# Grouping full-array and 64-column matmuls of two attention steps into one: a cross-attention and mixture-of-experts kernel

## Chip, cores and metric

One core of a Trainium2 chip (trn2). The metric is device time in microseconds of one execution, as the median of several runs. All times below are microseconds unless they are marked ns. Engines: PE is TensorE, DVE VectorE, ACT ScalarE, POOL GpSimd, and SP the engine whose queue issues most of the transfers.

## What is computed

All arrays are fp32. `x` is 16 batches of 100 rows of 256; `ctx_768` is 16 batches of 361 rows of 192.

```python
def _L0_xattn_ref(x, y, Wq, Wkv, Wproj, bproj):        # H, DK = 16, 64
    q = (x @ Wq).reshape(b, lq, H, DK).transpose(0, 2, 1, 3)
    kv = (y @ Wkv).reshape(b, lkv, 2, H, DK).transpose(2, 0, 3, 1, 4)
    k, v = (kv[0], kv[1])
    atten = jax.nn.softmax(jnp.einsum('bhid,bhjd->bhij', q, k) * SCALE, axis=-1)
    res = jnp.einsum('bhij,bhjd->bhid', atten, v)
    return res.transpose(0, 2, 1, 3).reshape(b, lq, H * DK) @ Wproj + bproj
...
x = x + _L0_xattn_ref(_layernorm(x, axis=-1), ctx_768, ...)
x = x + _L0_ffn_ref(_layernorm(x, axis=-1), ...)
```

`_L0_ffn_ref` is a SwiGLU of inner size 704 that all tokens share, plus one of 7 experts of the same size for each token, chosen by a sigmoid router. The change does not touch it.

## The kernel before

The 1600 tokens are 13 tiles of 128 rows (the last has 64), in groups for the layer norms. `acc` holds x, `xT` the transposed normalised rows. Behind the attention come the shared FFN's remaining groups, the sorting of tokens by expert, and 15 expert tiles; nothing of that is edited.

**Steps.** Attention runs over 32 steps `(b, g)`: 16 batches `b`, each with a first step `g = 0` (heads 0 to 7) and a second `g = 1` (heads 8 to 15). In a step, `scores` (L612) makes four pairs of products of queries with keys (L618): two heads at a time, in the upper and the lower 64 rows of the array, each into its own PSUM bank. For each pair `exponentials` (L629) takes row maxima on DVE (L631) and exponentials with sums on ACT (L634); `turning` (L642) then takes reciprocals (L644) and turns 32 x 32 blocks on DVE (L647) into `tb`. It runs one pair behind the scores, so that the last pair is turned at the end of the step. `moved` (L658) copies the sums' row to DRAM and back (`row`, `over`) and regroups `tb` to `aT` with 16 transfers (L668), half from SP's queue and half from POOL's. One step later `values` (L680) multiplies `aT` with the values `v` (L689: two heads side by side, in 64 columns of the array each) and DVE scales the result into `resT` (L704).

**Other PE work in the steps.** First steps have the batch's three value pairs (`value_pairs` L589, products at L551), second steps the next batch's four key pairs (`key_pairs` L562, also L551). Both are row-tiled: two products of 64 rows side by side. Each pair leaves a `put` that copies two PSUM banks to SBUF, by ACT, or by ACT and DVE. Queries are made for two batches at a time in four units (`q_units` L518, matmul L527, copy by DVE L534). `project` (L711, matmul L716) multiplies `resT` of a finished tile with Wproj and adds it to `acc` (L719). A group's layer norm is a list of small parts for DVE: moments (L171, L172) per tile, roots (L176, and L177 on POOL), normalisation (L182) per tile. Its `turn` (L196) transposes the tiles on PE (L202) and copies them to `xT` on ACT (L205). The router's logits are L232. These use the whole array.

**What orders the work.** PE, ACT, DVE and SP are scheduled by hand in the attention: each engine executes in the order of the calls. Deques feed the steps. `norms` holds layer-norm and router parts (`part`, L745, runs one: after the turned pairs in the step, and one at the end), `turns` holds transposes, `fillers` projections and router calls, `puts` the copies out of PSUM. The loop over the steps (L780) takes from them at fixed places. `load_later` (L488) issues weights and tiles of x by step number, and normalises tiles whose x has come. All PE outputs share one pool of 8 PSUM banks, `ps`, taken in turn, so a product waits until the bank used eight banks earlier has been read. `ap2` gives two buffers to `aT`, `tb`, `over`, `v` and `cT`, three to `kT`.

The functions that the diff touches, and those around them:

Of the kernel before, what the change touches and what calls it, by code (L numbers as in the profile page):

```python
# [22 lines left out]
B, LQ, C = 16, 100, 256  # L23
# [11 lines left out]
QB, QR = 4, 25  # L35
# [9 lines left out]
WE = 2 * 2 * I + (NI + 1) * C  # L45
QG = 2
HG = 8
WARM = 7
ZERO = 8
SAME = 3  # L50
EPS = 1e-5
# [3 lines left out]
def xattn_moe(  # L55
# [16 lines left out]
    nc = tc.nc  # L72
# [381 lines left out]
    with ExitStack() as attn:  # L454
# [22 lines left out]
        cTs = {0: load_ctx(0, NR)}  # L477
# [29 lines left out]
        for i in range(NA):  # L507
            at = aw.tile([P, 2, NJ * P], F32, name=f"at{i}")
            nc.gpsimd.memset(at[:, :, LKV:], 0.0)
            ats.append(at)  # L510
        for i in range(2):
            qT = aw.tile([P, NCH, QG * QB, 32], F32, name=f"qT{i}")
            nc.gpsimd.memset(qT, 0.0)
            qT_bufs.append(qT)

        qTs, kTs, vs, resTs = {}, {}, {}, {}
# [1 line left out]
        def q_units(g):  # L518

            qT = qT_bufs[g % 2]  # L520
            qTs[g] = qT

            def unit(u):
                pq = bank()[:, : 2 * QG * LQ].rearrange("p (o n) -> p o n", o=2)
                for o in range(2):
                    for k in range(2):
                        nc.tensor.matmul(  # L527
                            pq[:, o, :],
                            wq_sb[:, u, k, ts(o, P)],
                            xT[:, k, ts(g, QG * LQ)],  # L530
                            start=(k == 0),
                            stop=(k == 1),
                        )
                nc.vector.tensor_scalar(  # L534
                    qT[:, 2 * u : 2 * u + 2, :, :QR],
                    pq.rearrange("p o (i n) -> p o i n", n=QR),
                    DK**-0.5,
                    None,
                    ALU.mult,
                )  # L540

            return [lambda u=u: unit(u) for u in range(NU)]
# [19 lines left out]
        def key_pairs(b):  # L562
            cT = cTs[b]
            halves = []
            kTs[b] = halves

            def keys(u):


                def operands(o, k):  # L570
                    r = ts(o, P // 2)
                    return wk_sb[r, u, k, :], cT[r, k, :LKV]

                if u % 2 == 0:
                    halves.append(ap2.tile([P, 4, LKV], F32, name="kT", bufs=3))
                kT = halves[u // 2]
                to = pair(operands, P, LKV)

                def put():
                    c = 2 * (u % 2)  # L580
                    nc.scalar.copy(kT[:, c, :], to[0][:, :LKV])
                    one = nc.scalar.copy if u % 2 else nc.vector.tensor_copy
                    one(kT[:, c + 1, :], to[1][:, :LKV])

                return put

            return [lambda u=u: keys(u) for u in range(NU)]

        def value_pairs(b):  # L589
            cT = cTs.pop(b)  # L590
            v = ap2.tile([P, NJ, H * DK], F32, name="v")
            vs[b] = v

            def values_of(j):
                n = keys_in(j)

                def operands(o, k):
                    r = ts(o, P // 2)
                    return cT[r, k, ds(j * P, n)], wv_sb[r, k, :]

                to = pair(operands, n, 512)

                def put():
                    nc.scalar.copy(v[:n, j, :512], to[0][:n, :])
                    one = nc.vector.tensor_copy if j == 1 else nc.scalar.copy
                    one(v[:n, j, 512:], to[1][:n, :])

                return put

            return [lambda j=j: values_of(j) for j in range(NJ)]  # L610
# [69 lines left out]
        def values(b, g, aT, over):  # L680

            n2 = HG // 2
            av = bank()[:, : n2 * LQ].rearrange("p (c n) -> p c n", n=LQ)
            for i in range(n2):
                c = g * n2 + i
                for j in range(NJ):
                    n = keys_in(j)
                    for o in range(2):
                        nc.tensor.matmul(  # L689
                            av[ts(o, DK), i, :],  # L690
                            vs[b][:n, j, ds((2 * c + o) * DK, DK)],
                            aT[:n, :, j, o, ts(i, QR)],
                            start=(j == 0),
                            stop=(j == NJ - 1),
                        )
            blocks = av.rearrange("p c (i n) -> p c i n", n=QR)
            for t in range(b * LQ // P, ((b + 1) * LQ - 1) // P + 1):

                i0 = max(0, t * P - b * LQ) // QR
                i1 = (min(LQ, (t + 1) * P - b * LQ) + QR - 1) // QR  # L700
                if t not in resTs:
                    resTs[t] = ap2.tile([P, NCH, QP + P + QP], F32, name="resT")
                to = resTs[t][:, ts(g, n2), ds(QP + b * LQ + i0 * QR - t * P, (i1 - i0) * QR)]
                nc.vector.tensor_tensor(  # L704
                    to.rearrange("p c (i n) -> p c i n", n=QR),
                    blocks[:, :, i0:i1, :],
                    over[:, i0:i1].rearrange("p i c n -> p c i n"),
                    ALU.mult,
                )
# [13 lines left out]
        turns, fillers, norms = deque(), deque(), deque()  # L723
# [21 lines left out]
        def part():  # L745
            if norms:
                norms.popleft()()

        def after_values():
            if biases:  # L750
                t = biases.popleft()
                nc.gpsimd.tensor_tensor(acc[:, t, :], acc[:, t, :], bp_sb, ALU.add)

        puts = deque()

        def product(pairs):

            puts.append(pairs.pop(0)())
            if len(puts) > 1:
                puts.popleft()()  # L760

        pairs = key_pairs(0)
        product(pairs)
        product(pairs)
        parts, turn_first = layer_norm(FIRST)
        for one in parts:
            one()
        product(pairs)
        product(pairs)
        turn_first()  # L770
        normalised(SECOND)
        qs = q_units(0)
        for _ in range(2):
# [2 lines left out]
        NG = H // HG  # L776
        n2 = HG // 2
        steps = [(b, g) for b in range(B) for g in range(NG)]
        held = None
        for s, (b, g) in enumerate(steps):  # L780
            if g == 0:
                pairs = value_pairs(b)
                if s == 0:
                    kept = [pairs.pop()]
                    ask = lambda: qs.pop(0)() or (lambda: None)
                    pairs[1:1] = [ask, ask]
            elif b + 1 < B:
                pairs = key_pairs(b + 1)
                if s == 1:
                    pairs = kept + pairs  # L790
                if (b + 1) % QG == 0:
                    qs = q_units((b + 1) // QG)
            else:

                hT0 = ap2.tile([P, NJ, H * DK], F32, name="v")
                hT0 = hT0.rearrange("p j n -> p (j n)")[:, : (NI + 1) * 3 * P]
                hT0 = hT0.rearrange("p (i n) -> p i n", i=NI + 1)
                first = hidden(GROUPS[0], hT0, ap2, 3 * P, SAME)
                pairs = [lambda: first.pop(0)() or (lambda: None) for _ in range(SAME)]
            tb = new_blocks()  # L800
            turning = None
            for i in range(n2):
                exponentials, then = scores(b, g * n2 + i)
                if puts:
                    puts.popleft()()
                exponentials()
                if turning:
                    turning(tb)
                    part()
                turning = then  # L810
                if pairs:
                    puts.append(pairs.pop(0)())
            while pairs:
                product(pairs)
            if puts:
                puts.popleft()()
            if turns:
                turns.popleft()()
            if s and fillers:
                fillers.popleft()()  # L820
            for _ in range(min(2, len(qs))):
                qs.pop(0)()
            turning(tb)
            part()
            if s:
                values(b1, g1, *held)
                after_values()
                if g1 == NG - 1:
                    finished(b1)
            held = moved(tb)  # L830
            b1, g1 = b, g
            if g == NG - 1 and b + 2 < B:
                cTs[b + 2] = load_ctx(b + 2)
            load_later(s)
# [6 lines left out]
            if fillers:  # L841
                fillers.popleft()()
        down(GROUPS[0][:2], hT0)
        values(b1, g1, *held)
        down(GROUPS[0][2:], hT0[:, :, 2 * P :])
        finished(b1)
        while fillers:
            fillers.popleft()()

# [196 lines left out]
```

## Time and profile before

| what | value |
|---|---|
| median of 3 runs | 731.54 (731.47 to 731.96) |
| profiled execution, its own time | 730.98 |
| its span on the core | 729.3 |
| mean granted PE clock | 0.998 |
| PE busy, DVE busy, ACT busy | 99%, 58%, 38% of the span |
| L551 PE, value products | 576 records, 131.6, mean 589 ns |
| L551 PE, key products | 768 records, 128.4, mean 465 ns |
| L618 PE, scores | 512 records, 103.1, mean 478 ns |
| L689 PE, attention times values | 1536 records, 75.2, mean 252 ns |
| L527 PE, queries | 256 records, 47.2, mean 337 ns |
| L716 PE, projection | 208 records, 47.8, mean 383 ns |
| L634 ACT, exponentials | 256 records, 142.1, idle before them 206.8, of which 206.6 for DVE nm L631 |

How to read it: an fp32 matmul stands as two records[...]. Records of row-tiled or column-tiled pairs overlap in time[...], so record lengths add up to more than the time they took; starts are the safer measure. "64\*128" after a matmul is the array's part that it uses, rows by columns. In a timeline line stand the start, the time covered, the engine, the line, the operation, output from input, and in brackets the engine's idle time before it with what ended it. In a table of windows each engine has its busy time and its number of instructions; PEclk is the clock granted to PE as a share of full speed, then come the share of time of the DMA engines and GB/s.

### The profile page before, as it was taken

Reading aid. Unit: us, or ns where it says so; the run is one execution under the profiler, and the core shown is the slowest. Engines: PE = TensorE matmul, PEld = TensorE weight load, DVE = VectorE, ACT = ScalarE, POOL = GpSimd, SP = SyncE. Lnnn points to the kernel's source line nnn. Section 1 sums busy time; section 2 is a strip of 40 time slices with the busy share of each in tenths; the row PEclk is TensorE's granted clock in tenths of the full one; section 3 lists DMA queues with packets and bytes.
Section 4 is the critical chain, followed back from the end, with each engine's and each line's share of the span. In section 5 each row is a group of like instructions: output and inputs, shape, how many; then the busy total and the mean of one; then the engine's idle time right before and its main releaser. Section 6 shows DMA issues by size and latency. Waiting matters only on the chain. (4 is left out here: it accounts for less than half of the span.)

```text
span 729.3 us, 14750 instructions
## 1 busy us (share of the span) xinstructions
PE 721.5 (99%) x5206; PEld 516.7 (71%) x5206; DVE 421.2 (58%) x1086; ACT 280.3 (38%) x795; POOL 201.7 (28%) x418
## 2 busy tenths in 40 slices
PE   9999999999999999999999999999999999999996
PEld 6667666676666767576676666756767678999996
DVE  2877668568786866857866695776247222222221
ACT  2554556344544544534534463453021101112111
POOL 5242322323323222422223322223020102543221
PEclk9999999999999999999999999999999999999999
DMA  7164655534655553644534554445103901888860
GB/s 256 47 153 113 178 138 134 129 98 127 174 148 126 147 134 85 162 111 126 137 85 126 119 157 111 109 97 121 58 26 109 419 32 48 317 334 344 308 255 23
DMA packets 54375, 107.95 MB, mean 148 GB/s; under 512 B 28631, under 2 KB 35930, under 8 KB 52368
## 3 DMA queue, kind: packets, MB, share of 16 engines
q1 hardware_dynamic: 43648, 80.51, 36.4%
q0 software_dynamic: 10352, 25.98, 14.2%
q8 instruction: 44, 0.72, 0.4%
q14 instruction: 43, 0.35, 0.2%
q10 hardware_dynamic: 288, 0.39, 0.2%
HBM read 60.39 MB, written 5.35 MB: 90 GB/s over the span
## 5 line engine op out<-in xcount | busy, mean ns | idle before, releaser
L634 ACT ACTIVATE at<-mm,nm 128x361 f32<-128x361 f32 x256 | 142.1, 561 | 206.8 <-DVE nm L631 206.6
L668 POOL DMA_DIRECT2D aT<-tb x256 | 126.4, 501 | 300.1 <-PE mm L689 168.4
L631 DVE TENSOR_REDUCE nm<-mm 128x1 f32<-128x361 f32 x256 | 124.0, 526 | 50.9 <-PE mm L618 49.7
L647 DVE STREAM_TRANSPOSE tb<-at 128x384 f32<-128x384 f32 x256 | 132.9, 558 | 4.8 <-DMA aT<-tb 0.6
L551 PE MATMUL mm<-wv_sb,cT 64*128 64x512 f32 (+1 forms) x576 | 131.6, 589 | 0.0
L551 PE MATMUL mm<-cT,wk_sb 64*128 64x361 f32 x768 | 128.4, 465 | 0.0
L551 PEld LDWEIGHTS mm<-cT,wk_sb 64*128 64x128 f32 x768 | 76.3, 188 | 41.4 <-issue 0.5
L618 PE MATMUL mm<-kT,qT 64*128 64x361 f32 x512 | 103.1, 478 | 0.0
L551 PEld LDWEIGHTS mm<-wv_sb,cT 64*128 64x128 f32 (+1 forms) x576 | 53.9, 181 | 57.3 <-issue 46.5
L929 PE MATMUL mm<-xgT,wex 128*128 128x128 f32 x660 | 78.3, 275 | 0.5 <-ACT xgT L922 0.5
L929 PEld LDWEIGHTS mm<-xgT,wex 128*128 128x128 f32 x660 | 76.9, 192 | 1.4 <-issue 0.7
L689 PEld LDWEIGHTS mm<-aT,v 128*64 128x64 f32 (+1 forms) x1536 | 68.9, 135 | 10.6 <-issue 10.6
L689 PE MATMUL mm<-aT,v 128*64 128x100 f32 (+1 forms) x1536 | 75.2, 252 | 0.0
L618 PEld LDWEIGHTS mm<-kT,qT 64*128 64x128 f32 x512 | 46.6, 185 | 38.7 <-issue 14.4
L402 PE MATMUL mm<-xT,w_sb 128*128 128x384 f32 (+1 forms) x176 | 60.9, 503 | 0.0
L402 PEld LDWEIGHTS mm<-xT,w_sb 128*128 128x128 f32 x176 | 32.9, 190 | 25.7 <-issue 8.5
L634 ACT ACTIVATION_READ_ACCUMULATOR at<-mm,nm 128x1 f32 x256 | 50.4, 197 | 0.0
L527 PE MATMUL mm<-xT,wq_sb 128*128 128x200 f32 x256 | 47.2, 337 | 0.7 <-ACT xT L205 0.7
L716 PE MATMUL mm<-wp_sb,resT 128*128 128x256 f32 (+1 forms) x208 | 47.8, 383 | 0.0
L527 PEld LDWEIGHTS mm<-xT,wq_sb 128*128 128x128 f32 x256 | 43.0, 190 | 4.7 <-issue 2.0
L716 PEld LDWEIGHTS mm<-wp_sb,resT 128*128 128x128 f32 (+1 forms) x208 | 37.7, 186 | 9.9 <-ACT at L634 2.5
L941 PE MATMUL mm<-wex,hgT 128*128 128x256 f32 x180 | 41.4, 380 | 0.0
(139 smaller groups left out, 555.2 us busy)
## 6 DMA issues: line engine op xcount, KB each, us to landing
wex<-in_wex SPq DMA_DIRECT2D x15, 2176.0 KB
aT<-tb POOLq DMA_DIRECT2D x256, 80.2 KB, 3.1
aT<-tb SPq DMA_DIRECT2D x256, 80.2 KB
cT<-in_ctxT SPq DMA_DIRECT2D x15, 541.5 KB
over<-row SPq DMA_DIRECT2D x64, 100.0 KB
xn_d<-xn SPq DMA_DIRECT2D x12, 128.0 KB
base_d<-acc SPq DMA_DIRECT2D x12, 128.0 KB
w_sb<-in_w SPq DMA_DIRECT2D x4, 352.0 KB
```

The source lines that it names most:

```text
L402: nc.tensor.matmul(to[:, :n], w13_sb[:, k, ds(at, P)], xT[:, k, ds(g[0] * P, n)], start=(k == 0), stop=(k == 1),)
L527: nc.tensor.matmul(pq[:, o, :], wq_sb[:, u, k, ts(o, P)], xT[:, k, ts(g, QG * LQ)], start=(k == 0), stop=(k == 1),)
L551: nc.tensor.matmul(to[o][:height, :width], *operands(o, k), start=(k == 0), stop=(k == NR - 1),)
L618: nc.tensor.matmul(sc[o][:, :LKV], qTs[b // QG][r, c, ts(b % QG, QB), :], kTs[b][c // 4][r, c % 4, :], start=True, stop=True,)
L631: nc.vector.tensor_reduce(nm[:, o : o + 1], sc[o][:, :LKV], AX.X, ALU.max, negate=True)
L634: nc.scalar.activation(at[:, o, :LKV], sc[o][:, :LKV], AF.Exp, bias=nm[:, o : o + 1], accum_out=sums[:, o : o + 1],)
L647: nc.vector.transpose(tb[:, :, :, o, i * QR : i * QR + 32].rearrange("p j k n -> p k j n"), at[:, o, :].rearrange("p (k j n) -> p k j n", ...
L668: queue.dma_start(aT[ts(j, 32), i].rearrange("p k o n -> p (k o n)"), tb[ts(i, 32), j].rearrange("p k o n -> p (k o n)"),)
L689: nc.tensor.matmul(av[ts(o, DK), i, :], vs[b][:n, j, ds((2 * c + o) * DK, DK)], aT[:n, :, j, o, ts(i, QR)], start=(j == 0), stop=(j == NJ ...
L716: nc.tensor.matmul(pp[:r, :C], resT[:, c, QP : QP + r], wp_sb[:, c, :], start=(c == 0), stop=(c == NCH - 1))
L929: nc.tensor.matmul(to[:, ts(o, P)], w[:, ds(j * 2 * I + u, P)], xgT[:, j, :], start=(j == 0), stop=(j == 1),)
L941: nc.tensor.matmul(y[:, :C], hT[:, c, :], w[:, ds(4 * I + c * C, C)], start=(c == 0), stop=(c == NI))
```

## The change

It moves calls in the step loop and edits what feeds them:

- Queries, transposes, projections, router logits and the values products now stand only at the end of first steps. There `values` runs for both steps of the batch in front, one after the other (`held` keeps two sets of `aT` and `over`). Second steps have scores, key pairs and value pairs only.
- Of a batch's three value pairs, two are made in the second step of the batch in front, put among its key pairs; the third stays behind the first scores of the batch's first step. Batch 0 makes all three in its first step.
- With more pairs than scores in a step, pairs are spread over the remaining scores, and a pair's `put` is called at the next pair.
- Transposes still run at most once a step, `fillers` until none is left; the query units of batches 2k and 2k+1 are made in the first steps of batches 2k-1 and 2k.
- In the first two steps up to three layer-norm parts run at the end of the step instead of one.
- Ahead of the steps, the first transposes stand before the fourth key pair instead of behind it, one of seven warm-up matmuls goes, and POOL clears only the padding columns of `qT`.
- In the last step no projection is made; tile 10's is made after it, and both of batch 15's values blocks stand together in the tail.

```diff
-WARM = 7
+WARM = 6
...
-            nc.gpsimd.memset(qT, 0.0)
+            nc.gpsimd.memset(qT[:, :, :, QR:], 0.0)
...
         def value_pairs(b):
-            cT = cTs.pop(b)
+            cT = cTs[b]
...
         product(pairs)
+        turn_first()
         product(pairs)
-        turn_first()
         normalised(SECOND)
...
-        held = None
+        held = []
+        values_of = {b: value_pairs(b) for b in (0, 1)}
         for s, (b, g) in enumerate(steps):
             if g == 0:
-                pairs = value_pairs(b)
+                pairs = values_of.pop(b)
                 if s == 0:
-                    kept = [pairs.pop()]
                     ask = lambda: qs.pop(0)() or (lambda: None)
-                    pairs[1:1] = [ask, ask]
+                    pairs[1:] = [ask, ask] + pairs[1:]
+                elif (b + 1) % QG == 0 and b + 1 < B:
+                    qs = q_units((b + 1) // QG)
             elif b + 1 < B:
+                if b:
+                    values_of[b + 1] = value_pairs(b + 1)
                 pairs = key_pairs(b + 1)
-                if s == 1:
-                    pairs = kept + pairs
-                if (b + 1) % QG == 0:
-                    qs = q_units((b + 1) // QG)
+                for i in (4, 2):
+                    pairs.insert(i, values_of[b + 1].pop(0))
...
                 turning = then
-                if pairs:
-                    puts.append(pairs.pop(0)())
-            while pairs:
-                product(pairs)
+                for _ in range(-(-len(pairs) // (n2 - i))):
+                    product(pairs)
             if puts:
                 puts.popleft()()
-            if turns:
-                turns.popleft()()
-            if s and fillers:
-                fillers.popleft()()
-            for _ in range(min(2, len(qs))):
-                qs.pop(0)()
+            if g == 0:
+                if turns:
+                    turns.popleft()()
+                while fillers:
+                    fillers.popleft()()
+                for _ in range(min(2, len(qs))):
+                    qs.pop(0)()
             turning(tb)
-            part()
-            if s:
-                values(b1, g1, *held)
-                after_values()
-                if g1 == NG - 1:
-                    finished(b1)
-            held = moved(tb)
-            b1, g1 = b, g
+            for _ in range(3 if s < 2 else 1):
+                part()
+            if g == 0 and s:
+                for at in range(NG):
+                    values(b - 1, at, *held.pop(0))
+                    after_values()
+                finished(b - 1)
+            held.append(moved(tb))
...
         down(GROUPS[0][:2], hT0)
-        values(b1, g1, *held)
+        for at in range(NG):
+            values(B - 1, at, *held.pop(0))
         down(GROUPS[0][2:], hT0[:, :, 2 * P :])
-        finished(b1)
+        finished(B - 1)
```

## What the change is expected to do

> **What bounds the kernel now.** I read the busy shares first, then TensorE's timeline step by step, then VectorE and ScalarE in the same stretches, last the waits. The page:
>
> ```profile
> PE 721.5 (99%) x5206; PEld 516.7 (71%) x5206; DVE 421.2 (58%) x1086; ACT 280.3 (38%) x795; POOL 201.7 (28%) x418
> PEclk9999999999999999999999999999999999999999
> ```
>
> TensorE (PE) is busy throughout at full clock. So a change can gain only where PE streams less densely, and every wait it puts on PE counts whole. PE's timeline in one first step (here without queries):
>
> ```profile
> 349.73 2.35 PE L689 MATMUL mm<-aT,v 128*64 128x100 f32 x48
> 352.00 0.88 PE L618 MATMUL mm<-kT,qT 64*128 64x361 f32 x4
> 352.71 2.74 PE L551 MATMUL mm<-wv_sb,cT 64*128 64x512 f32 x12
> 355.29 0.77 PE L618 MATMUL mm<-kT,qT 64*128 64x361 f32 x4
> 355.89 2.74 PE L551 MATMUL mm<-wv_sb,cT 64*128 64x512 f32 x12
> ...
> 361.65 0.77 PE L618 MATMUL mm<-kT,qT 64*128 64x361 f32 x4
> 362.36 2.35 PE L689 MATMUL mm<-aT,v 128*64 128x100 f32 x48
> ```
>
> Starts matter. Scores before a value pair take 0.60 (355.29 to 355.89), as inside a row-tiled run. Before L689 they take 0.71 (361.65 to 362.36), after L689 0.71 too (352.00 to 352.71). The excess appears wherever the array's tiling changes: R = 64 rows (L551, L618), C = 64 columns (L689), F = full (L202, L527, L716, L232, L402). From single records' starts (a slot is one record, or the two that run side by side): L689's slots are 0.088 apart, but 0.181 lie between its last and L618's first; L618's are 0.303 apart, but its first two after a change 0.408. So leaving a mode costs about 0.095 and the first slot of the next 0.105 more (0.055 for L689 and L202): 0.15 to 0.20 a change.
>
> Now the engines behind scores, at the end of a first step:
>
> ```profile
> 332.57 0.77 PE L618 MATMUL mm<-kT,qT 64*128 64x361 f32 x4
> ...
> 333.37 0.97 DVE L631 TENSOR_REDUCE nm<-mm 128x1 f32<-128x361 f32 x2 [1.03 <-PE mm L618]
> 334.00 0.56 ACT L634 ACTIVATE at<-mm,nm 128x361 f32<-128x361 f32 x1 [0.16 <-DVE nm L631]
> 334.26 0.16 DVE L644 RECIPROCAL at<-sums 128x2 f32<-128x2 f32 x1
> ...
> 335.00 0.20 ACT L634 ACTIVATION_READ_ACCUMULATOR at<-mm,nm 128x1 f32 x1
> ...
> 338.12 0.16 DVE L644 RECIPROCAL at<-sums 128x2 f32<-128x2 f32 x1
> 338.31 1.04 DVE L647 STREAM_TRANSPOSE tb<-at 128x384 f32<-128x384 f32 x2
> 339.27 0.14 DVE L250 TENSOR_SCALAR lg<-lg 128x21 f32<-128x21 f32 x1
> ```
>
> This gives the units: reduction starts 0.80 after the scores; a reduced pair occupies DVE 0.89 (333.37 to 334.26); a turned pair 1.15 (338.12 to 339.27); ACT's exponentials end 1.83 after the reduction's start (335.20).
>
> **What is removed.** In the new instruction order, mode changes fall from 103 to 67. C to R 30 to 15 at 0.20 (-3.0); R to C 9 to 0 at 0.15 (-1.35); F to C 25 to 18 at 0.15 (-1.05); R to F 28 to 23 (0.20 each, 0.15 to L202, 0.12 to L232) -0.93; F to R one more and C to F one fewer cancel. Sum **-6.3**. The number of matmuls is unchanged but for one warm-up.
>
> At the start, xT's wait goes:
>
> ```profile
> 13.27 0.59 ACT L205 COPY xT<-mm 128x512 f32<-128x512 f32 x1 [1.95 <-PE mm L202]
> 13.91 2.97 PE L527 MATMUL mm<-xT,wq_sb 128*128 128x200 f32 x16 [0.68 <-ACT xT L205]
> ```
>
> A key pair (1.82) now covers it. But the transposes, moved up to 10.8, meet the second L182, done at 11.16: new wait 0.25, plus a mode change already counted. Queries start near 13.58: **-0.3**. The dropped warm-up is worth nothing, since this L182 sets the resumption; without that cover 0.2 [...]. The smaller qT memset is off every path (old one done at 9.54, scores at 16.81).
>
> **What is moved, and who gets late.** In a first step, three scores now stand back to back behind one value pair (2.58). Let 0 be the step's start: scores at 0, 3.18, 3.79, 4.39; PE reaches the full-array work at 5.1. DVE's order is reduce 1, turn 0, norm part, reduce 2, turn 1, norm part, reduce 3, turn 2. Reduce 1 starts at 3.98, turn 0 ends 6.02; without parts reduce 2 ends 6.91, turn 1 8.06, and ACT has exponentials 3 at 9.89. L205's copy stands behind those on ACT, and L182 inside that DVE chain. Before, scores were spread through the step and neither was late. A transposed tile costs PE 0.22, L716 3.46, L182 0.40, a moments part (L171, L172) 0.55, copy to matmul 0.64 (13.27 to 13.91). I resolved the semaphores on which these PE instructions wait in the new program:
> - Batch 1: queries wait for the xT copy just made: 9.95+0.64=10.6, PE ready at 6.05: 4.5.
> - Batch 5: same, two moments parts delay it to 11.7; L716 brings PE to 9.3: 2.4.
> - Batch 6: the fourth transpose waits for L182 after turn 0 (6.5, not 5.8): 0.7.
> - Batch 7: one L182 in the chain; the router's L232 waits for xT until 11.0, PE ready at 9.3: 1.7.
> - Batches 10 and 14: the third transpose waits for the L182 after turn 1: 6.02+0.40+0.89+1.15+0.40=8.86, with handover 8.95; PE there at 5.6: 3.35 each, 6.7.
> Sum **+16.0**. These are lower-bounded by DVE's own busy time, hence ±1.5.
>
> Other queues. aT's copy, from row issue to landing, took 7.5 to 8.5 in every step. The second step now ends with a value pair instead of L689, so the row leaves 1.1 after the next step starts and lands at 8.6 to 9.6; the second L689 block comes at 8.75 in batch 15 (no queries): 0 to 0.9, taken 0.4. Batch 2 has 10.2: free. SP's next ctx transfer lands about 12.1 after the row against a need at 13.1: 0 to 0.3, taken 0.1. The first half's aT copy now waits on SP and POOL for its buffer's L689 at the step's end; behind it stand over, ctx and L177, none needed for several us: nothing. In second steps a value pair adds 0.69 to DVE and 1.77 to ACT, but DVE's 11 and ACT's 10.6 stay below PE's 14.9: nothing. At the tail L716 moves behind L402, still covered: nothing. Waits: **+16.5**.
>
> **The clock.** Nothing in the stretch shows what such idle gaps do to PE's clock (its largest gap here is 0.68). Nearest is the end of the run:
>
> ```profile
> 720.00:724.00 4.00, 3.76 (x18) 2.97 (x16) 0.69 (x2) 0.00 (x0) 0.99 (x1) 1.00 0.11 39
> 724.00:729.00 5.00, 0.00 (x0) 0.00 (x0) 0.28 (x1) 0.00 (x0) 0.98 (x1) 0.70 0.08 26
> ```
>
> PE stops at 723.76; a mean of 0.70 over the next row is full clock for 2.0 and half for 3.0, so the clock halves near 726.0, 2.3 after the last matmul. [...] By the row, batch 1 triggers it and batches 10 and 14 (3.35 with 0.2 of transposes inside) mostly, batch 5 sometimes. [...] I take the row, as measured on this program: 1.6+1.2+1.2=**+4.0**; ends 0 and 8.
>
> **Sum.** -6.3-0.3+16.5+4.0=+13.9. The profiled execution took 730.98 (span 729.3), so its like would take 744.9; the median of runs is 731.54, giving **745.4**.
>
> **Rivals.**
> - Waits as worked out, clock stays full: +9.9, 741.4. [...]; against: the tail row. 0.20.
> - Waits hidden, so only mode changes count: 731.54-6.6=724.9, faster. Mechanism: reductions and turns fall behind by less, so that L205 and L182 are done when PE reaches 5.1. It decides if DVE could finish the chain above 3.4 to 4.5 sooner. Against: 3.98 is set by PE itself, and six DVE pieces follow in order at measured lengths. 0.05. Partial cover ending within 0.2%: 0.02.
> - Mode changes do not pay (cost remains inside the longer runs) or more waits and clock drops than listed: +20 to +25, 751.5 to 756. For it: DVE's lag may carry over; against: second steps leave it 4 us of slack. 0.11.
> - As forecast, 740 to 751: 0.62.
>
> A measurement here can tell about 0.2% from no change. Faster by more 0.05, within 0.02, slower 0.93. The range runs from below the full-clock case to just into the worst: 739.5 to 752.
>
> **What would show it.** Right: PE idle of about 4.5 before L527 near batch 1, 2.4 at batch 5, waits at L202 in batches 10 and 14, L232 in batch 7, named by ACT xT or DVE xn; PEclk below 9 right after; no idle between the two L689 blocks but in batch 15; second steps of 14.9 without a mode change. Wrong: no PE idle there, or VectorE's chain done before 5.1; then the time falls towards 725.

## The result, and the profile after

The changed kernel takes 750.79 us (median of 6 runs, 746.50 to 753.46), the kernel before, run beside it, 731.50: a ratio of 1.0258, 95% interval 1.0228 to 1.0289. It is slower by 19.3. The profiled execution took 748.78 with a span of 747.1; that of before had 730.98 and 729.3. The forecast, 745.4, had the sign and nearly all of the mechanism; the time is 5.4 above it and inside the range.

First the busy line and the row of the granted clock, from the page after:

```profile
PE 723.4 (97%) x5204; PEld 525.3 (70%) x5204; DVE 421.5 (56%) x1086; ACT 282.6 (38%) x795; POOL 198.6 (27%) x418
PEclk9999999999999999999999999999999999999999
```

TensorE's busy time is 1.9 more than before and the span 17.8 more, so most of the loss is idle time on TensorE. The clock's row reads 9 in all forty slices, as it did before, where the prediction expected less: a slice is 18.7 us here, 3.41 of them at 0.50 still leave a mean of 0.91, and a 9 stands for 0.90 or more. What TensorE waited for, as total, number of times and longest:

```profile
PE mm L202 <- DVE xn L182: 7.3, 6, 2.0
PE mm L527 <- ACT xT L205: 5.8, 2, 3.9
PE mm L689 <- DMA over<-row: 1.3, 1, 1.3
...
PE mm L551 <- ACT at L634: 0.8, 1, 0.8
...
PE mm L232 <- ACT xT L205: 0.5, 1, 0.5
PE mm L551 <- DMA cT<-in_ctxT: 0.4, 1, 0.4
```

Before, the only one of these lines was 0.7 for L527. Now there are 16 us of them. The largest, in the timeline of batch 1's first step (start, duration, engine, and in brackets the idle time before and who ended it):

```profile
51.81 1.09 PE L202 MATMUL mm<-ident,xn 128*128 128x128 f32 x8
...
54.46 0.94 DVE L631 TENSOR_REDUCE nm<-mm 128x1 f32<-128x361 f32 x2
...
55.05 0.56 ACT L634 ACTIVATE at<-mm,nm 128x361 f32<-128x361 f32 x1 [0.81 <-DVE nm L631]
...
56.14 1.07 ACT L205 COPY xT<-mm 128x512 f32<-128x512 f32 x2
56.77 4.66 PE L527 MATMUL mm<-xT,wq_sb 128*128 128x200 f32 x16 [3.87 <-ACT xT L205]
```

TensorE had finished the transposes by 52.9. The copies to xT stand on ScalarE behind the last score pair's exponentials, and those follow a reduction that VectorE reached only at 54.46. The queries themselves then take 4.66 for 16 records, against 2.97 in the row of before. The windows of the same trace show why; the columns are busy time (and instructions) of TensorE, its weight loads, VectorE, ScalarE and POOL, then the granted clock, the DMA share and GB/s:

```profile
54.19:57.61 3.42, 0.84 (x5) 0.84 (x6) 2.31 (x6) 2.21 (x7) 0.00 (x0) 1.00 0.88 196
57.61:61.02 3.41, 3.41 (x12) 3.41 (x11) 0.58 (x1) 0.00 (x0) 0.00 (x0) 0.50 0.16 64
...
180.48:183.89 3.41, 1.63 (x10) 1.63 (x11) 2.31 (x7) 1.94 (x6) 0.00 (x0) 1.00 0.56 176
```

In the stretch that holds the wait TensorE was busy for 0.84 of 3.42; in the next one the clock is 0.50. The third line holds batch 5's wait, with 1.63 busy, and no drop followed it. In the whole run the clock stood at 0.50 for 3.41 at batch 1 and for 6.83 at batch 14, and again from 743.68 to the end, after TensorE's last matmul. TensorE was idle for 0.74 of those 10.24; I count half of the rest, 4.7 us, as lost work. The other five executions had a mean clock of 0.987 to 0.994, this one 0.991, and their times differ with it: 746.50 at 0.994, 753.46 at 0.988.

### The profile page after: what moved, and what is told of

Its sections match the earlier page's. It is cut to its first block, busy times and chain, and to the rows that moved or that the text cites. A ratio compares the mean times of both kernels' runs of the same rounds, so it can differ in the third digit from the quotient of the medians.

```text
span 747.1 us, 14777 instructions
## 1 busy us (share of the span) xinstructions
PE 723.4 (97%) x5204; PEld 525.3 (70%) x5204; DVE 421.5 (56%) x1086; ACT 282.6 (38%) x795; POOL 198.6 (27%) x418
## 5 line engine op out<-in xcount | busy, mean ns | idle before, releaser
L634 ACT ACTIVATE at<-mm,nm 128x361 f32<-128x361 f32 x256 | 141.6, 559 | 188.0 <-DVE nm L631 187.9
L551 PE MATMUL mm<-wv_sb,cT 64*128 64x512 f32 (+1 forms) x576 | 133.3, 589 | 0.8 <-ACT at L634 0.8
L618 PE MATMUL mm<-kT,qT 64*128 64x361 f32 x512 | 98.4, 471 | 0.0
L551 PEld LDWEIGHTS mm<-wv_sb,cT 64*128 64x128 f32 (+1 forms) x576 | 56.4, 180 | 56.3 <-issue 43.7
L618 PEld LDWEIGHTS mm<-kT,qT 64*128 64x128 f32 x512 | 49.8, 186 | 35.1 <-issue 8.4
L689 PE MATMUL mm<-aT,v 128*64 128x100 f32 (+1 forms) x1536 | 72.8, 251 | 1.3 <-DMA over<-row 1.3
L689 PEld LDWEIGHTS mm<-aT,v 128*64 128x64 f32 (+1 forms) x1536 | 69.2, 135 | 5.4 <-issue 3.2
L527 PE MATMUL mm<-xT,wq_sb 128*128 128x200 f32 x256 | 48.6, 344 | 5.8 <-ACT xT L205 5.8
L527 PEld LDWEIGHTS mm<-xT,wq_sb 128*128 128x128 f32 x256 | 45.0, 196 | 9.2 <-ACT xT L205 6.5
L716 PE MATMUL mm<-wp_sb,resT 128*128 128x256 f32 (+1 forms) x208 | 50.4, 398 | 0.0
L716 PEld LDWEIGHTS mm<-wp_sb,resT 128*128 128x128 f32 (+1 forms) x208 | 39.8, 196 | 10.0 <-issue 2.4
L581 ACT COPY kT<-mm 128x361 f32<-128x361 f32 x64 | 29.4, 461 | 45.1 <-PE mm L551 45.1
```

Source lines behind the costliest of these rows:

```text
L527: nc.tensor.matmul(pq[:, o, :], wq_sb[:, u, k, ts(o, P)], xT[:, k, ts(g, QG * LQ)], start=(k == 0), stop=(k == 1),)
L551: nc.tensor.matmul(to[o][:height, :width], *operands(o, k), start=(k == 0), stop=(k == NR - 1),)
L618: nc.tensor.matmul(sc[o][:, :LKV], qTs[b // QG][r, c, ts(b % QG, QB), :], kTs[b][c // 4][r, c % 4, :], start=True, stop=True,)
L634: nc.scalar.activation(at[:, o, :LKV], sc[o][:, :LKV], AF.Exp, bias=nm[:, o : o + 1], accum_out=sums[:, o : o + 1],)
L689: nc.tensor.matmul(av[ts(o, DK), i, :], vs[b][:n, j, ds((2 * c + o) * DK, DK)], aT[:n, :, j, o, ts(i, QR)], start=(j == 0), stop=(j == NJ ...
L716: nc.tensor.matmul(pp[:r, :C], resT[:, c, QP : QP + r], wp_sb[:, c, :], start=(c == 0), stop=(c == NCH - 1))
```

## Experiments

Theory 1, as in the prediction: score pairs standing back to back make VectorE and ScalarE late, TensorE waits where it reads what is queued behind them, and the waits halve the clock. Rival (theory 2): the waits come from putting transposes and their readers into one step, whatever the spacing of the scores. Some expectations name a third, that VectorE's lateness holds TensorE up wherever the work stands. A second pair of theories, A and B, is about the clock. The changes of tiling that the expectations name (99, 63, 79) leave out four around the last short tile's L716, which all kernels share; the prediction's 103 and 67 have them.

**Value pairs back in the first step.** One part of the change undone:

```
                 pairs = key_pairs(b + 1)
-                for i in (4, 2):
-                    pairs.insert(i, values_of[b + 1].pop(0))
```

> The changed kernel with one part undone: all three value pairs of a batch stand in its first step again, one behind each score pair, and the second step has the keys only; the full-array work and both value-product blocks stay in the first step. The number of changes of tiling is that of the changed kernel. Theory 1 (the three scores standing back to back make VectorE and ScalarE late, and TensorE waits for them): the waits at batches 5, 6, 7, 10 and 14 go, also the 0.84 in the second step of batch 0 and the 1.28 at batch 15; at batch 1 some 2.5 of 4 stay, since the queries follow their own transposes at once. The time is 727.6, between 725 and 730, faster than the kernel before. Theory 2 (the waits come from turning the tokens in the same step as the work that reads them, whatever the spacing): the waits at batches 1, 5, 7 stay nearly whole and so do the clock drops, 740 or more.

Measured: 727.59 against 731.83, ratio 0.9941 (0.9922 to 0.9960), clock 0.998. Of the waits that the change brought, two are left:

```profile
PE mm L527 <- ACT xT L205: 1.1, 1, 1.1
PE mm L618 <- ACT at L634: 0.8, 1, 0.8
```

The order still has the transposes, projections and both value-product blocks in the first step, so theory 2 falls. Batch 1 keeps 1.11 rather than the 2.5 I expected. The 0.84 in step 0,1 did not go: it is not due to the value pairs. The trace shows VectorE standing in front of a part (L182) that waits for POOL's power (L177, 33.33 to 34.38), with a reduction queued behind it:

```profile
34.42 0.41 DVE L182 TENSOR_SCALAR xn<-acc,mv,rstd 128x256 f32<-128x256 f32 x1 [1.49 <-POOL rstd L177]
```

The three parts at the end of the first two steps put it there; in the best version below two parts run there, and the wait is gone.

**Two value pairs in the first step, one in the second.** A smaller dose of the same part:

```
-                for i in (4, 2):
-                    pairs.insert(i, values_of[b + 1].pop(0))
+                pairs.insert(4, values_of[b + 1].pop(0))
```

> Between the changed kernel and spread: two value pairs stand in the first step and one in the second, so that two score pairs stand back to back at the first step's end, not three. The 63 changes of tiling stay. Theory 1 with the units of the prediction (reduced pair 0.89, turned pair 1.15, part 0.40): TensorE reaches the full-array work at 7.7, the third reduction starts at 9.2; waits of 2.5 at batch 1, 0 to 0.3 at batch 5, 1.4 each at batches 10 and 14, none at 6 and 7; with the 0.84, 0.4 and 1.3 that do not hang on the scores, some 8 in all, and hardly a clock drop, since none reaches half a window but that of batch 1: 734.5 (731 to 738). Theory 2 (a wait does not depend on how many scores stand together, only on whether any do): 745 or more. If the wait vanishes with two (threshold below three): 729.

Measured: 732.19 against 730.89, ratio 1.0020 (1.0011 to 1.0030), clock 0.999.

```profile
PE mm L202 <- DVE xn L182: 2.8, 2, 1.4
PE mm L527 <- ACT xT L205: 2.3, 1, 2.3
```

L202 waits 1.39 at batch 10 and 1.40 at batch 14, worked out as 1.4 each; L527 waits 2.32 at batch 1, worked out as 2.5. The units of VectorE's chain size the waits for two scores as for three, and the 745 of theory 2 is far off. The profiled run has no drop of the clock and none of the 1.3 for aT, and the time is 2.3 less than expected. (Four of the other thirteen executions have a mean clock of 0.993 to 0.996, so some of them did drop.)

**The move of the value pairs alone.** The kernel before, with its value pairs distributed as in the changed kernel and nothing else:

```
...
-                pairs = value_pairs(b)
+                pairs = values_of.pop(b) if b in values_of else value_pairs(b)
...
+                if b:
+                    values_of[b + 1] = value_pairs(b + 1)
+                    for i in (4, 2):
+                        pairs.insert(i, values_of[b + 1].pop(0))
...
-                if pairs:
-                    puts.append(pairs.pop(0)())
-            while pairs:
-                product(pairs)
+                for _ in range(-(-len(pairs) // (n2 - i))):
+                    product(pairs)
```

> The kernel before with one part of the change alone: two of a batch's three value pairs stand in the second step of the batch in front, among the keys, so that three score pairs stand back to back in the first step; full-array work and value products stay in both steps. 99 changes of tiling as before. Nearly all transposes and their readers then fall into second steps, where the scores are spread. Theory 1 (a wait needs clustered scores and, right behind them, work that reads what VectorE or ScalarE has queued after them): waits only at batch 1 and batch 7, at most 4 and 1, with at most one clock drop: 733 (731 to 736). Theory 3 (the late VectorE holds up TensorE whatever follows, through banks or aT): 740 or more.

Measured: 767.14 against 730.89, ratio 1.0488 (1.0436 to 1.0539), clock 0.980. My expectation of 733 was wrong by 34. The largest wait of the trace and one of its ten places:

```profile
PE mm L689 <- DMA over<-row: 24.7, 10, 4.3
```

```profile
183.19 1.99 PE L618 MATMUL mm<-kT,qT 64*128 64x361 f32 x12
188.42 3.92 PE L689 MATMUL mm<-aT,v 128*64 128x100 f32 x48 [3.23 <-DMA over<-row]
```

The step began near 179.9, and its scores were through at 185.2, since two of the three value pairs that had filled it stand elsewhere. The value products that follow read aT, whose copy was issued behind the row's, at 179.34; in the kernel before, its last packet landed 7.4 to 8.6 after the row's issue in every step, which would be 186.7 to 187.9 here, and L689 started at 188.42. So I take it that in a first step with nothing but one value pair and scores, L689 waits for that copy. (The releaser named, over, was issued behind aT's copy on SP's queue; L689 does not read it.) The 48 records at 188.42 then took 3.92, against 2.35 at 177.63, and the run's mean clock is 0.980, against 0.998 before. Six of the ten places are of this kind, the longest wait 4.3; in the other four, queries stand in between, as at 156.02, where the wait is 1.50. In the changed kernel the projections and the first half's value products stand ahead of the second half's, which covers the copy everywhere but at batch 15 (1.28). The time that theory 3 named came, but not by its mechanism: VectorE had turned the last pair by 179.31, before the step began, so it was not late; TensorE came sooner. The parts of the change are not a sum: moving the value pairs alone costs 36, and the other parts cover most of what it uncovers.

**Value-product blocks joined alone.** The kernel before, with both L689 blocks of a batch in the next first step:

```
...
-            if s:
-                values(b1, g1, *held)
-                after_values()
...
-            held = moved(tb)
+            if g == 0 and s:
+                for at in range(NG):
+                    values(b - 1, at, *held.pop(0))
+                    after_values()
+                finished(b - 1)
+            held.append(moved(tb))
```

> The kernel before with one part of the change alone: both value-product blocks of a batch (L689) stand in the next batch's first step, one behind the other. Everything else, full-array work in both steps too, stays. The changes of tiling go from 99 to 79 by the order of the matmuls (from C to R 15 fewer at 0.20, into C 16 fewer at 0.15, from full to R 12 more at 0.20). If a change of tiling costs what I read from single starts, 3.0 less: 728.5 (727 to 730), and no wait. Rival: the cost stays inside the longer runs and the time is within 0.2% of before (730 to 733). Rival: the second half's aT comes late and the time rises above 733.

Measured: 729.35 against 731.83, ratio 0.9971 (0.9961 to 0.9981): 2.5 less (1.4 to 2.9 by the interval) for 20 fewer changes of tiling, or 0.12 each, where I had worked out 3.0, and no new wait. So the changes of tiling that this run leaves out did cost time.

**The transposes earlier.** In the changed kernel, with each router behind its transposes as before:

```
...
                 for _ in range(-(-len(pairs) // (n2 - i))):
                     product(pairs)
+                if i == 0 and g == 0 and turns:
+                    turns.popleft()()
...
-                if turns:
-                    turns.popleft()()
```

> The changed kernel with the transposes (L202, L205) moved: they stand in the first step behind its first value pair, no longer at the step's end; where the normalisation is not finished by then, one batch later. The scores stay clustered. Theory 1 (a wait arises only where TensorE needs something that was queued behind the clustered scores on VectorE or ScalarE) and theory 2 (the turn stands too close to its readers) both say that the waits at batches 1, 5, 6, 7, 10 and 14 go (15.5) with the clock drops (about 5 in the profiled run), against 12 more changes of tiling (2.1): 730.8, between 728 and 734, about the kernel before. If the delay of VectorE were not tied to the order in the step (theory 3), the waits would move to other lines and the time stay above 740.

Measured: 735.56 against 731.83, ratio 1.0061 (1.0043 to 1.0079). The waits for L182 and L205 are gone at all six batches, and with them some 15 us. It is 4.8 above the expectation. In the profiled run (clock 0.997) that is one new wait, 1.75 at batch 7, some 1.7 in the slower records behind it, by my estimate, and 1.14 at the start, where the first context's transfer landed late; the last is of unknown cause. The wait at batch 7:

```profile
229.48 0.41 DVE L182 TENSOR_SCALAR xn<-acc,mv,rstd 128x256 f32<-128x256 f32 x1 [4.08 <-PE mm L202]
...
232.57 2.99 PE L618 MATMUL mm<-kT,qT 64*128 64x361 f32 x8 [1.75 <-ACT at L634]
```

VectorE stood for 4.08 in front of an L182 that waits for the transposes. It reached the next reduction only at 231.25, behind a turned pair and another L182, and a score pair waits for the exponentials behind that reduction. Behind the wait, 8 records of L618 took 2.99, against 1.99 for 12 in the changed kernel at 496.66, and 16 of L716 took 4.75, against 3.62 there at batch 5. The waits did not all move elsewhere, so theory 3 is not the cause in the changed kernel; but clustered scores leave little room for anything between them.

**TensorE kept busy in the waits.** Matmuls whose results are overwritten, in the changed kernel; the first form:

```
...
+    def keep_busy(to, n):
+        for _ in range(n):
+            nc.tensor.matmul(to[:, :C], ident, wq_sb[:, 0, 0, :], start=True, stop=True)
...
                 tr = bank()
+                if keep and i and tiles[0] in (3, 6):
+                    keep_busy(tr, 7)
...
+                if u == 0 and g in (1, 3):
+                    keep_busy(pq, 14 if g == 1 else 6)
```

> The changed kernel with matmuls added that compute nothing used: 14 of 128x256 before the queries of batch 1, 6 before those of batch 5, 7 before the third tile's transposes of batches 10 and 14, written to the bank that the real matmuls overwrite. They take less than the wait they stand in, so the waits end when they did. Theory A (the clock is halved because TensorE is idle in these waits): the granted clock returns to 0.998, no half-rate stretch inside the run, and the time falls by what the half rate costs, to about 743.5 (742 to 745). Theory B (the clock drops for another reason, or the waits are longer than the idle time shown): the time stays near 750, or rises.

Measured: 749.04 (ratio 1.0246, 1.0226 to 1.0267) with a clock of 0.998 in the profiled run, 0.996 to 0.999 in the others. The clock obeyed theory A, the time theory B, because I had counted an added matmul as one record: it is two. The 28 records ahead of batch 1's queries kept TensorE to 58.56, 6.0 after the transposes, where the wait was 3.87. Inconclusive on the time. The same with 7, 3 and 4 added matmuls:

> As clock_fill, with half as many added matmuls (7 before the queries of batch 1, 3 before those of batch 5, 4 before the third tile of batches 10 and 14), since each 128x256 one turned out to be two records of 0.216: clock_fill's 6.0, 2.6, 3.0 and 3.0 outlasted the waits they stood in (3.87, 1.96, 1.97, 1.98). Now 3.0, 1.3, 1.7 and 1.7 fit inside. Theory A (idle TensorE halves the clock): clock 0.998, the time falls against the changed kernel by what half rate costs: 743.5 (742.5 to 745). Theory B (something else keeps it slow): 748 or more.

Measured: 742.81, ratio 1.0164 (1.0149 to 1.0178), four executions within 0.7, clock 0.998 or 0.999. No half-rate stretch is left inside the run; the window that holds the start of batch 1's queries is now

```profile
55.48:58.89 3.41, 2.93 (x18) 2.69 (x18) 0.82 (x2) 0.92 (x2) 0.00 (x0) 1.00 0.45 154
```

Theory A holds for this kernel: with the waits partly filled the mean clock is 0.998 instead of 0.988, and the half rate costs the changed kernel some 7 to 8 of its 19 (8.0 by the medians, about 7 by the two ratios). The other 11 to 12 are waits less the gain of fewer changes of tiling.

**Pauses of graded length.** In the kernel before, at the end of 14 second steps:

```
...
+        def pause(n):
+            to = bank()
+            nc.tensor.matmul(to[:, :P], ident, ones, start=True, stop=True)
+            nc.scalar.copy(still[:, 0], to[:, :P])
+            for i in range(2 * n):
+                nc.scalar.copy(still[:, 1 - i % 2], still[:, i % 2])
+            nc.tensor.matmul(to[:, P : 2 * P], still[:, 0], ones, start=True, stop=True)
...
+            if g and 0 < b < B - 1:
+                pause((b - 1) % 7)
```

> The kernel before with a pause of TensorE at the end of each second step from batch 1 to 14: a matmul, then a chain of copies on ScalarE, then a matmul that reads the last copy; none of it is used. The chain has 1, 3, 5, 7, 9, 11 and 13 copies, twice over, so that the idle times run from about 1.3 to 5. If the clock follows the share of idle time in a window of 3.4 (theory A: windows with 1.3 or less idle keep it, with over 2.1 lose it, as the changed kernel's trace shows), then pauses under 1.7 never halve the clock, those over 3.5 always do, and those between do according to where the window falls, for one or two windows each. [...] If it were the 2.3 after the last matmul (my row), all above 2.3 do.

Measured, in one execution: 791.33, clock 0.977. Three of its stretches at 0.50 begin at 176.34, 248.02 and 387.97, the second and third 21 and 62 times 3.41 after the first; those of the changed kernel at 57.61 and 463.79, 119 times 3.41 apart. Four pauses of the ladder, each with the window that holds its idle time, or the larger part of it, and the next one or two:

```profile
172.93:176.34 3.41, 1.38 (x8) 0.98 (x10) 0.05 (x1) 1.79 (x6) 3.08 (x7) 1.00 0.85 213
176.34:179.76 3.42, 3.42 (x10) 1.37 (x8) 0.92 (x2) 1.19 (x4) 0.00 (x0) 0.50 0.82 192
...
244.61:248.02 3.41, 0.13 (x1) 0.13 (x2) 0.00 (x0) 2.94 (x10) 3.39 (x8) 1.00 0.83 210
248.02:251.44 3.42, 3.42 (x10) 1.79 (x12) 0.98 (x2) 0.75 (x3) 0.43 (x1) 0.50 0.88 203
251.44:254.85 3.41, 3.41 (x20) 1.67 (x18) 0.81 (x2) 1.76 (x5) 0.00 (x0) 1.00 0.98 271
...
384.56:387.97 3.41, 1.74 (x28) 1.41 (x23) 2.78 (x13) 2.02 (x7) 1.49 (x4) 1.00 0.11 25
387.97:391.38 3.41, 3.41 (x12) 1.69 (x12) 0.97 (x2) 1.07 (x4) 2.44 (x5) 0.50 0.91 233
...
422.10:425.51 3.41, 1.76 (x10) 1.18 (x12) 0.44 (x1) 1.47 (x5) 2.85 (x6) 1.00 0.90 228
425.51:428.92 3.41, 3.41 (x19) 1.55 (x17) 1.20 (x4) 2.37 (x7) 0.00 (x0) 1.00 0.83 188
```

After a pause of 1.67 that fell within one window (1.74 busy) the next stood at 0.50; after one of 2.33 that the grid divided into 0.69 and 1.64 (1.76 busy in the second window) it stood at 1.00. The two with 1.38 and 0.13 busy were followed by 0.50. In the changed kernel those with 0.84 and 1.26 busy were followed by 0.50, those with 1.63 (batch 5) and 1.78 (batch 10) by 1.00. So of these windows, those with 1.38 busy or less were followed by a drop and those with 1.76 or more were not; of the two in between, 1.63 kept the clock and 1.74 lost it, and what decides there was not measured. Of the windows at 0.50, the one with 0.74 idle (463.79, changed kernel) was followed by a second; those at 57.61 there and at 248.02 in the ladder, without idle time, were followed by 1.00.

**The start alone.** The kernel before with the change's order at the start:

```
+        turn_first()
         product(pairs)
-        turn_first()
```

and WARM = 6.

> The kernel before with the change's start alone: the first transposes a key pair earlier, and 6 instead of 7 warm-up matmuls. If the wait for xT before the queries goes (0.68) and the second normalised tile comes 0.25 late, with one change of tiling more: 0.3 less, 731.5 against 731.8. Rival: [...]: no difference.

Measured: 730.59 against 730.93, ratio 0.9998 (0.9990 to 1.0006). It cannot decide: the interval holds 0.3 less as well as no change. (By the order of its matmuls this kernel has two more changes of tiling than before, not one as I expected.)

**The best version.** Value pairs as in the first experiment, and

```
+                if s == 2 and i == 0:
+                    turns.popleft()()
...
-            for _ in range(3 if s < 2 else 1):
+            for _ in range(2 if s < 2 else 1):
```

> As spread (value pairs all in the first step), and two more edits: the transposes of batch 1 stand behind the first value pair of that step (its 1.11 before the queries goes, two changes of tiling come, 0.35), and two instead of three parts of the normalisation at the ends of the first two steps (so that a reduction does not queue on VectorE behind a part that waits for POOL's power in step 0,1: 0.84). By these terms 1.3 to 1.9 less than spread: 726 (725 to 727.5), faster than both kernels. Rival: the waits reappear elsewhere in the start, 727.6 as spread or more.

Measured: 724.47 against 730.93, ratio 0.9912 (0.9899 to 0.9925), faster than both kernels, and 0.5 below the range I had given. What its trace names as waited for by TensorE, in full:

```profile
PE mm L122 <- DVE ones L119: 1.1, 1, 1.1
PE mm L934 <- ACT xgT L927: 0.5, 1, 0.5
```

With no wait left that the kernel before does not have, the remainder is the prediction's first term: 34 fewer changes of tiling, worked out as 6.0, and the start's 0.3, against 6.5 measured. That is 0.18 a change against 0.12 in the run with joined blocks; the two runs remove different kinds of change, and why the prices differ was not measured.

## Why the prediction was right, and where it was off

- **Fewer changes of tiling, -6.3:** right in size. By themselves 20 of them were worth 2.5 (computed: 3.0), and in the best version all but two of the change's, with the start, 6.5 (computed: 6.3).
- **Start, -0.3:** in the trace the queries came 0.38 earlier (13.53 against 13.91); alone it can't be told from nothing.
- **Waits at six batches, +16.0:** the places and the lines were right, but for 0.79 before a transpose (L202) at batch 7, where only the router's L232 was named, and for the waits of batches 10 and 14, which come in two pieces each. The idle times are 3.87 at batch 1 (worked out: 4.5), 1.96 at batch 5 (2.4), 0.72 at 6 (0.7), 1.32 in two pieces at 7 (1.7, in one), 2.89 at each of 10 and 14 (3.35): 13.7 in nine pieces. An idle time between records understates the delay: a record of L527 lasts 0.33, but the starts in a run lie 0.17 apart, so 0.16 more is lost each time (0.27 and 0.11 for L202), which makes 15.1. The size follows VectorE's chain, as two scores instead of three show.
- **Waits outside the scores' reach, +0.5:** 2.5 measured as idle time (3.0 with 0.16 for each of the three). aT of batch 15 was 1.28 rather than 0.4: its last packet landed 7.7 after the issue, within what I took, but L689 started 1.6 later still; I had put the landing and the use at one time. The context's transfer at batch 2 took 0.41 instead of 0.1. The 0.84 in step 0,1 was missed: I had followed the edits of the value pairs and not that three norm parts in place of one put L182, which waits for POOL, ahead of a reduction.
- **Clock, +4.0:** this is the term that made the forecast short. The profiled run lost 4.7, the median run 7 to 8, as its mean clock says too (0.988 against 0.998 before, which is 7.5 of 750). The step that failed is my reading of the row, "the clock halves near 726.0, 2.3 after the last matmul". The time after the last matmul does not order what the traces show: a pause of 2.33 left the clock at 1.00, while one of 1.67 within one window of 3.41 was followed by 0.50. The end of the kernel before, in the windows below, fits the share of a window: 1.18 busy of 3.41, and 0.50 follows. The size, 1.6 and twice 1.2, was an estimate of mine: no trace that I had then showed how long the clock stays at 0.50. That 4.0 came near 4.7 is partly luck: I had put one drop at each of batches 1, 10 and 14, and the trace has one window of 3.41 at 1, none at 10 and two at 14.

```profile
722.58:725.99 3.41, 1.18 (x6) 0.70 (x4) 0.48 (x1) 0.00 (x0) 1.21 (x2) 1.00 0.13 43
725.99:729.26 3.27, 0.00 (x0) 0.00 (x0) 0.00 (x0) 0.00 (x0) 0.16 (x1) 0.50 0.10 35
```

- **The rivals:** full clock (741.4) is what the half-filled waits gave, 742.8, so that rival's sum was right and its premise wrong. Waits hidden (724.9) is what the best version gave, 724.5, once the scores were spread.
- **The sum:** in the profiled run -6.6 for tiling and start as worked out, 15.1 and 3.0 for the waits and 4.7 for the clock make 16.2 of the 17.8 by which the span grew; 1.6 is not accounted for.

What stays open: why 1.78 idle kept the clock at batch 5 where 1.67 lost it in the ladder, the price of each kind of change of tiling, and the late first transfer in one run.

## What to carry to other kernels

Count what a step holds between two users of a slow engine: taking filler matmuls out of a step can be free by TensorE's sum and still bring scores together whose reductions, exponentials and transfers need that time, and everything behind them in those queues becomes late. When TensorE must wait, look at the granted clock behind the wait as well: here the profiled run lost about 18 in the waits and, by my count, another 4.7 at a clock of 0.50. Undo one part of a change at a time: in this case one part alone was worth -2.5, another alone +36, and the change without the second -4.

## What the hardware showed that I had not expected

In the ladder the clock dropped after a window that was only half idle (1.67 of 3.41). Two equal waits of the changed kernel in different batches (2.89 at batches 10 and 14, the same to 0.01) cost differently: after the one the clock stayed at 1.00 and the 16 records of L716 took 3.62, after the other it stood at 0.50 for 6.83 and they took 6.41. What I see to differ is how the windows of 3.41 divided the idle time: 1.26 and 1.63 in the one, 2.15 and 0.74 in the other, as TensorE's busy time of each window, the first after the length, shows:

```profile
334.09:337.50 3.41, 2.15 (x14) 0.94 (x10) 3.22 (x9) 2.12 (x7) 1.75 (x4) 1.00 0.92 259
337.50:340.91 3.41, 1.78 (x10) 1.63 (x11) 3.34 (x10) 2.28 (x9) 0.00 (x0) 1.00 0.55 133
...
460.38:463.79 3.41, 1.26 (x8) 0.40 (x4) 3.34 (x10) 2.28 (x8) 0.86 (x2) 1.00 0.85 248
463.79:467.21 3.42, 2.67 (x8) 2.26 (x9) 2.60 (x7) 1.95 (x7) 0.00 (x0) 0.50 0.65 127
```

An f32 matmul of 128x256 stands in the traces of this case as two records whose starts lie 0.216 apart (L716 in the kernel before).
